# The way down of layer 0 by seven block products instead of eight, with the right operands kept in DRAM

## The chip, the core and the metric

The kernel runs on one NeuronCore of one Trainium2 chip. The time is that of one execution on the device, in microseconds (us). Three runs of the kernel before took 2002.38, 2007.29 and 2008.54 us; the median is 2007.29.

The engines are named as the profile names them: PE is TensorE (matmul), PEld its loading of the stationary operand, DVE is VectorE, ACT is ScalarE, POOL is GpSimd. SP is SyncE, whose queue (SPq) issues most of the transfers. Each engine takes its instructions strictly in the order in which the program lays them down for it.

## What is computed

Two transformer layers over x of shape (4, 512, 512), in float32. Each is x + attention(norm(x)) + ffn(norm(x)). The part that the change touches is the feed-forward half of layer 0, beside its attention, which is a scan over 32 steps of 16 tokens (test-time training: each step makes a gradient and updates the state W1 and b1).

```python
def _L0_ffn_ref(x, gate_w, up_w, down_w, gate_s, up_s, down_s):
    # here x: (2048, 512); gate_w, up_w: (1408, 512); down_w: (512, 1408)
    g = jnp.einsum('th,ih->ti', xf, gate_w) * gate_s
    u = jnp.einsum('th,ih->ti', xf, up_w) * up_s
    hdn = jax.nn.silu(g) * u
    out = jnp.einsum('ti,hi->th', hdn, down_w) * down_s
...
def step(carry, x):                      # layer 0's attention, 32 of these in a chain
    Z1 = xk @ W1_s + b1_s
    grad = _ln_fused_l2_bwd(Z1, xv - xk, ln_w, ln_b)
    ...
    W1_new = W1_s - (last_eta * xk).swapaxes(-1, -2) @ grad
```

The results must agree with this reference; the order of the sums is free.

## The kernel before

Layer 0 is one loop of 32 scan steps with other work laid between. The 2048 tokens fall into 8 chunks of 256 (CW), and a chunk holds 4 scan steps. For every chunk there is a stream of other work, the generator `between(ch)` (L656):

- `gate_up` (L465), 11 times: the inner width of 1408 is 11 tiles (NI) of 128. Each loads a gate tile and an up tile (wg, wu, 256 KB each, L471), makes 4 + 4 products of 128x256 into one PSUM bank (pf, two banks), and leaves silu(gate) x up in `hid` (ACT L477, DVE L478). `hid` has one buffer.
- the next chunk's work: `norm_turn`, `keys`, two `token_tile`s and `queries`. `token_tile` writes the step's rows to DRAM by 8 transfers each on SP (L294).
- `finish` of the chunk before: its norm, the output projection and the sum with the result of the way down.
- `down` (L483), twice, for the two halves u of 128 tokens: for each of the 11 inner tiles it loads a tile of the down weights (wd, 128x512, 256 KB, four buffers, L489) and makes one product of 512 columns, which accumulates in one PSUM bank (pd). DVE then multiplies by the row of scales `dsc` (L494), and POOL adds `brow` and x (L495, L496).

One scan step n is: `prepare` on POOL (kv fetched from DRAM, L307; sk, L314; the query part of wq_bd, L316; km, L321); on PE the products pz and then pso from wh; the gradient, a chain of some fifteen small operations on DVE with two on ACT (L356 to L390); its copies g_bd (L395, DVE and ACT), and gh on POOL (L421); then on PE the products wacc (from g_bd) and pso (from a_bd and gh), which open the next step. `fill(us)` (L702) draws pieces of `between` into the gaps of the scan by their estimated length (the numbers that the generators yield), and a step that needs a later chunk waits until that chunk's rows are made. The tile framework's planner then orders the instructions of each engine by when it expects their operands. So what stands on PE between a step's pz and its wacc or pso is fixed in the program.

In the first chunk `finish_constants` (L515) also runs: it spreads the row `dsc` over the partitions by one product of 512 columns, and makes `brow` from the output weights.

`down` and what draws it:

Of the kernel before, what the change touches and what calls it, by code (L numbers as in the profile page):

```python
# [18 lines left out]
P = 128  # L19
# [13 lines left out]
NS = 8  # L33
# [22 lines left out]
def trunk_kernel(ctx: ExitStack, tc: tile.TileContext, a: dict, out: bass.AP):  # L56
# [49 lines left out]
    with ExitStack() as px:  # L106
# [9 lines left out]
        def mm(out, lhsT, rhs, start=True, stop=True):  # L116
            nc.tensor.matmul(out, lhsT=lhsT, rhs=rhs, start=start, stop=stop, skip_group_check=True)  # L117
# [67 lines left out]
        gamma_row = wk.tile([P, HS], F32, tag="xr", name="gamma_row")  # L185
# [15 lines left out]
        tok = lrb[:, P:]  # L201


        sel8 = one.tile([NS, P], F32, tag="sel8", name="sel8")
        tok8 = one.tile([NS, 2, 4, HD], F32, tag="tok8", name="tok8")
        for h in range(2):
            r = slice(4 * h, 4 * h + 4)
            nc.gpsimd.dma_start(
# [249 lines left out]

        gs = load(one, "gs", [P, NI], eng=nc.gpsimd)
        us = load(one, "us", [P, NI], eng=nc.gpsimd)  # L460
        dsc = one.tile([P, HS], F32, tag="dsc", name="dsc")
        nc.gpsimd.dma_start(out=row["dsc"], in_=a["dsc"].unsqueeze(0))
        hid, yf = {}, {}

# [36 lines left out]
        ch8 = one.tile([NS, 4, 32], F32, tag="ch8", name="ch8")  # L501
# [12 lines left out]

        def finish_constants():  # L515
            nc.sync.dma_start(out=wo, in_=a["wo"].rearrange("(c p) o -> p c o", p=P))
            spread_row(dsc, row["dsc"])
            pt = psum()[:, :NS]
            nc.tensor.transpose(pt, ch8.rearrange("s al x -> s (al x)"), ident[:NS, :NS])
            nc.vector.tensor_copy(by_ch, pt)  # L520
            yield 1.0

            pt = psum()[:, :NC]
            mm(pt, onesd, beta_ch)
            beta_m = wk.tile([P, 1], F32, tag="beta_m", name="beta_m", bufs=1)
            nc.vector.tensor_reduce(beta_m, pt, AX.X, ALU.add)
            nc.vector.tensor_scalar(beta_ch, beta_ch, beta_m, None, ALU.subtract)

            pr = psum()
            for c in range(NC):  # L530
                pnb_b = wk.tile([P, P], F32, tag="pnb_b", name=f"pnb_b{c}")
# [1000 lines left out]
```

## Time and profile before

| | us |
|---|---|
| median of 3 runs | 2007.29 |
| profiled execution, its own time | 2001.78 |
| its span | 2000.0 |
| layer 0 (until the last latents) | about 970 to 1000 |
| layer 0's way down: 352 records of 128x512 on PE | 166.3 |
| gate and up tiles: 704 + 704 records of 128x256 | 174.7 + 168.2 |
| POOL busy, 160 to 900 us | 271.51 of 740 |
| DVE busy, 160 to 900 us | 463.55 of 740 |
| mean granted clock of PE over the span | 0.995 |

How to read it: a product in float32 leaves two records on PE, so 352 records are 176 products. A group's line gives the busy time of all its instructions, the mean of one in ns, and behind the second bar the time that its engine stood idle just before them, with what ended that wait. A line number can be that of a helper: every product of layer 0 stands at L117 (`mm`). In the views in order of time a line begins with its start and its length, and the bracket behind it holds the idle time before it.

### The profile page before, as it was taken

The numbers are of one execution on the slowest core, as the hardware profiler recorded it, in microseconds if no ns is written. First come the engines' busy times: TensorE is split into PE (matmuls) and PEld (weight loads), VectorE is DVE, ScalarE is ACT, GpSimd is POOL, SyncE is SP. The second block draws the span as 40 slices with busy tenths as digits, with TensorE's granted clock in tenths as the row PEclk, the third lists the DMA queues.
The fourth block names the chain that finished last, engine by engine and source line by source line (L and its number), as shares of the span: only waits on it lengthen the run. The fifth ranks groups of instructions, "written<-read, shape, count | busy, mean of one in ns | idle before, by whom it ended". The sixth has DMA issues, their size and how long they took to land.

```text
span 2000.0 us, 32373 instructions
## 1 busy us (share of the span) xinstructions
PE 1939.4 (97%) x11626; PEld 1233.0 (62%) x11626; DVE 1170.9 (59%) x2579; ACT 815.8 (41%) x1695; POOL 515.9 (26%) x619
## 2 busy tenths in 40 slices
PE   8999999999999999998999999999999999999997
PEld 6777676767767676743777745555555555555555
DVE  5445757475666566574555566555655556555664
ACT  2224334334334342432222165554554455445552
POOL 4334343424243343412000101111211121322110
PEclk9999999999999999999999999999999999999999
DMA  6657566646465455746652144444444434333343
GB/s 167 199 138 212 143 188 169 181 115 192 123 172 167 124 175 152 229 117 200 224 167 63 44 112 127 123 102 109 105 103 107 106 102 112 93 97 97 102 107 103
DMA packets 227307, 273.50 MB, mean 137 GB/s; under 512 B 88587, under 2 KB 117452, under 8 KB 226508
## 3 DMA queue, kind: packets, MB, share of 16 engines
q1 hardware_dynamic: 206656, 239.28, 43.5%
q0 software_dynamic: 8992, 26.84, 4.7%
q10 hardware_dynamic: 11500, 5.32, 0.9%
q8 instruction: 93, 1.52, 0.3%
q14 instruction: 66, 0.54, 0.1%
HBM read 174.18 MB, written 34.87 MB: 105 GB/s over the span
## 4 chain that ended last, share of the span: by engine, by line
PE 49%; DVE 1%; DMA 1%; SPq 0%; ACT 0%; issue 0%; DVEq 0%; ACTq 0%
PE pc L1254 11%; PE sc L1207 9%; PE pq L1184 8%; PE px L1301 5%; PE p L1301 4%; PE pk L1184 3%; PE epg L976 3%; PE epo L1039 1%; PE epu L976 1%; PE eox L1069 1%; PE pvo L891 1%; PE pw L866 1%; PE eo L1069 1%; DMA gu<-in_gu 0%; SPq L1246 0%
## 5 line engine op out<-in xcount | busy, mean ns | idle before, releaser
L1225 DVE TENSOR_REDUCE st<-sc 128x1 f32<-128x512 f32 x256 | 168.9, 681 | 242.4 <-PE sc L1207 242.4
L1227 ACT ACTIVATE prob<-sc,st 128x512 f32<-128x512 f32 x256 | 175.1, 686 | 213.7 <-DVE st L1225 213.5
L1254 PE MATMUL pc<-prT,lv 128*128 128x512 f32 x512 | 232.5, 597 | 5.2 <-DMA out<-y 3.9
L1236 DVE STREAM_TRANSPOSE tt<-prob 128x512 f32<-128x512 f32 x256 | 178.4, 700 | 46.6 <-ACT prob L1232 37.1
L1232 ACT ACTIVATE prob<-prob,st 128x512 f32<-128x512 f32 x256 | 182.0, 720 | 58.2 <-DVE st L1231 58.2
L117 PE MATMUL pf<-xT,wg 128*128 128x256 f32 x704 | 174.7, 390 | 4.1 <-DMA wg<-in_wg 2.7
L1184 PE MATMUL pq<-cq,uq 128*128 128x512 f32 x384 | 175.2, 592 | 0.0
L117 PE MATMUL pf<-xT,wu 128*128 128x256 f32 x704 | 168.2, 382 | 0.9 <-DMA wu<-in_wu 0.7
L117 PE MATMUL pd<-wd,hid 128*128 128x512 f32 x352 | 166.3, 601 | 1.3 <-DMA wd<-in_wd 1.3
L1254 PEld LDWEIGHTS pc<-prT,lv 128*128 128x128 f32 x512 | 96.8, 191 | 106.8 <-issue 104.5
L117 PEld LDWEIGHTS pf<-xT,wg 128*128 128x128 f32 x704 | 133.1, 193 | 31.2 <-issue 4.9
L1207 PE MATMUL sc<-k,q 32*128 32x512 f32 x1024 | 145.7, 617 | 2.5 <-ACT prob L1227 2.5
L117 PEld LDWEIGHTS pf<-xT,wu 128*128 128x128 f32 x704 | 134.7, 192 | 20.7 <-DMA wu<-in_wu 2.1
L478 DVE SCALAR_TENSOR_TENSOR hid<-pf,us,sg 128x256 f32<-128x256 f32 x88 | 42.0, 478 | 155.3 <-ACT sg L477 154.9
L1184 PEld LDWEIGHTS pq<-cq,uq 128*128 128x128 f32 x384 | 74.1, 193 | 90.7 <-issue 89.7
L314 POOL TENSOR_SCALAR sk<-k,m 128x256 f32<-128x256 f32 x64 | 60.3, 952 | 180.9 <-PE pz L117 168.7
L1195 POOL TENSOR_TENSOR kr<-kr,t2k 128x512 f32<-128x512 f32 x16 | 20.3, 1268 | 332.3 <-DVE t2k L1194 332.3
L421 POOL TENSOR_SCALAR gh<-grad,m 128x256 f32<-128x256 f32 x64 | 61.9, 976 | 153.2 <-DVE grad L390 131.0
L117 PEld LDWEIGHTS pd<-wd,hid 128*128 128x128 f32 x352 | 63.3, 190 | 60.4 <-issue 44.2
L1207 PEld LDWEIGHTS sc<-k,q 32*128 32x128 f32 x1024 | 48.4, 185 | 82.8 <-issue 73.2
L477 ACT ACTIVATE sg<-pf,gs 128x256 f32<-128x256 f32 x88 | 41.6, 473 | 134.8 <-PE pf L117 134.5
L1256 ACT COPY ctxT<-pc 128x512 f32<-128x512 f32 x64 | 37.4, 584 | 132.0 <-PE pc L1254 132.0
(316 smaller groups left out, 3455.2 us busy)
## 6 DMA issues: line engine op xcount, KB each, us to landing
prT<-tt SPq DMA_DIRECT2D x1016, 64.0 KB, 2.0
wd<-in_wd SPq DMA_DIRECT2D x176, 256.0 KB, 3.1
wg<-in_wg SPq DMA_DIRECT2D x88, 256.0 KB, 3.1
wu<-in_wu SPq DMA_DIRECT2D x88, 256.0 KB, 3.0
cq<-lat_d SPq DMA_DIRECT2D x48, 256.0 KB, 3.8
rows<-rows SPq DMA_DIRECT2D x128, 66.0 KB, 2.2
kv<-rows POOLq DMA_DIRECT2D x32, 264.0 KB, 4.3
gu<-in_gu SPq DMA_DIRECT2D x3, 2048.0 KB
```

What stands on the lines that cost most here:

```text
L117: nc.tensor.matmul(out, lhsT=lhsT, rhs=rhs, start=start, stop=stop, skip_group_check=True)
L314: nc.gpsimd.tensor_scalar_mul(sk[:, :, :, h, :], at(k1[ch], slice(0, P)), m2[:, h : h + 1])
L421: nc.gpsimd.tensor_scalar_mul(gh[:, :, h, :], g, m2[:, h : h + 1])
L976: nc.tensor.matmul(ps, lhsT=w[:, c, :], rhs=x[:, c], start=start and c == 0, stop=c == 1, skip_group_check=True)
L1184: nc.tensor.matmul(ps, lhsT=columns(ws[hg][w]), rhs=x, start=(i == 0), stop=(i == len(srcs) - 1))
L1207: nc.tensor.matmul(ps[h], lhsT=qk[f"q{c}"][r, i * P : (i + 1) * P], rhs=qk[f"k{c}"][r, :], start=(n == 0), stop=(n == 2),)
L1225: pin(nc.vector.tensor_reduce(mx, ps[h], AX.X, ALU.max, negate=True))
L1227: pin(nc.scalar.activation(pr, ps[h], AF.Exp, bias=mx, scale=1.0, accum_out=sm))
L1232: pin(nc.scalar.mul(pr, pr, sm))
L1236: nc.vector.transpose(out=tt[:, :, h - 2], in_=pr.rearrange("p (k kq j) -> p kq k j", kq=4, j=32))
L1254: pin(nc.tensor.matmul(pc, lhsT=lv[:, b, k, :], rhs=at[:, :, k, :], start=(k == 0), stop=(k == E - 1)))
L1301: nc.tensor.matmul(ps[:, q, :], lhsT=a[:, k, q * P : (q + 1) * P], rhs=w[:, k, :], start=start and k == 0 and q == 0, stop=k == 1, skip_gr ...
```

## The change

The product of a chunk's hidden values (256 tokens by 1408) with the down weights (1408 by 512) is cut into a 2x2 by 2x2 block product over ten of the eleven inner tiles: the tokens into two halves of 128, the inner width into two halves of 5 tiles (KH), the output columns into two halves of 256 (half). Seven block products and sums of blocks take the place of eight. The eleventh tile is done directly, in four products of 128x256.

The right operands (three blocks as they are and four of their combinations, all already times `dsc`) are made once, during the first chunk's gate/up tiles, by `down_operands`: a piece after each of tiles 1 to 6. Each piece loads 128x2x512 of the weights (SP), multiplies by `dsc` (DVE, 128x1024), makes four differences of 128x256 (POOL) and writes the seven parts to `rights_d` in DRAM (SP, three transfers). Every chunk loads the seven operands from there, 640 KB each, into two buffers.

The left operands are two sums of 128x640 made by `left_sums` after the tenth gate/up tile, and two more made in place in `hid`, all on POOL. The seven products are made one after the other; four of them add to the same PSUM bank x without clearing it, so that the bank holds the running sum that the next output block wants, and DVE adds each result to `yf`, which already holds x (loaded at the fifth tile) and `brow`.

```diff
-        def down(ch, u):
-            xr = wk.tile([P, HS], F32, tag="xr", name=f"xr_{ch}_{u}")
-            load_rows(xr, a["x"], ch, u)
-            pd = ps_dn.tile([P, HS], F32, tag="pd", name=f"pd_{ch}_{u}")
-            for i in range(NI):
-                w = wk.tile([P, HS], F32, tag="wd", name=f"wd_{ch}_{u}_{i}", bufs=4)
-                nc.sync.dma_start(out=w, in_=a["wd"][i * P : (i + 1) * P, :])
-                mm(pd, hid[ch][:, i, u * P : (u + 1) * P], w, i == 0, i == NI - 1)
-                if i in (3, 7):
-                    yield 3.43
-            t = wk.tile([P, HS], F32, tag="yf", name=f"yf_{ch}_{u}", bufs=4)
-            nc.vector.tensor_mul(t, pd, dsc)
-            nc.gpsimd.tensor_add(xr, xr, brow)
-            nc.gpsimd.tensor_add(t, t, xr)
-            yf[ch, u] = t
-            yield 2.57
+        KH, half = NI // 2, HS // 2
+        rights_d = dram.tile([7, P, KH, half], F32, tag="rights_d", name="rights_d")
+
+        def down_operands():
+            dsc = wk.tile([P, HS], F32, tag="xs", name="dsc", bufs=3)
+            spread_row(dsc, row["dsc"])
+            nc.sync.dma_start(out=last_d, in_=a["wd"][2 * KH * P :, :])
+            nc.gpsimd.tensor_mul(last_d, last_d, dsc)
+            pairs = a["wd"][: 2 * KH * P].rearrange("(k i p) o -> i p k o", k=2, i=KH)
+            for i in range(KH):
+                raw = wk.tile([P, 2, HS], F32, tag=("zb", "pn_sq")[i % 2], name=f"wd_{i}", bufs=1)
+                nc.sync.dma_start(out=raw, in_=pairs[i])
+                nc.vector.tensor_mul(raw, raw, dsc.unsqueeze(1).to_broadcast([P, 2, HS]))
+                b11, b12, b21, b22 = (raw[:, k, o : o + half] for k in range(2) for o in (0, half))
+                t = wk.tile([P, KH, half], F32, tag="wd", name=f"td_{i}")
+                nc.gpsimd.tensor_sub(t[:, 0], b12, b11)
+                nc.gpsimd.tensor_sub(t[:, 1], b22, t[:, 0])
+                nc.gpsimd.tensor_sub(t[:, 2], b22, b12)
+                nc.gpsimd.tensor_sub(t[:, 3], b21, t[:, 1])
+                nc.sync.dma_start(out=rights_d[0][:, i], in_=b11)
+                nc.sync.dma_start(
+                    out=rights_d[1:3, :, i].rearrange("j p o -> p j o"), in_=raw[:, 1].rearrange("p (j o) -> p j o", j=2)
+                )
+                nc.sync.dma_start(out=rights_d[3:, :, i].rearrange("j p o -> p j o"), in_=t[:, :4])
+                yield
...
+        def residual(ch):
+            for u in range(2):
+                t = yf[ch, u] = wk.tile([P, HS], F32, tag="yf", name=f"yf_{ch}_{u}", bufs=4)
+                load_rows(t, a["x"], ch, u)
+
+        def left_sums(ch):
+            a11, a12, a21, a22 = (
+                hid[ch][:, k * KH : (k + 1) * KH, u * P : (u + 1) * P] for u in range(2) for k in range(2)
+            )
+            s = wk.tile([P, 2, KH, P], F32, tag="hs", name=f"hs_{ch}", bufs=1)
+            nc.gpsimd.tensor_add(s[:, 0], a21, a22)
+            nc.gpsimd.tensor_sub(s[:, 1], s[:, 0], a11)
+            left[ch] = dict(a11=a11, a12=a12, a21=a21, a22=a22, s1=s[:, 0], s2=s[:, 1])
+
+        def down(ch):
+            o = left.pop(ch)
+            def add(ps, u, oh):
+                t = yf[ch, u][:, oh * half : (oh + 1) * half]
+                nc.vector.tensor_add(t, ps, t)
+            def product(ps, x, j, start, more=None):
+                w = wk.tile([P, KH, half], F32, tag="wd", name=f"wd_{ch}_{j}")
+                nc.sync.dma_start(out=w, in_=rights_d[j])
+                for k in range(KH):
+                    mm(ps, x[:, k, :], w[:, k, :], start and k == 0, k == KH - 1 and more is None)
+                if more:
+                    last(ps, *more, False)
+            def last(ps, u, oh, start):
+                mm(ps, hid[ch][:, NI - 1, u * P : (u + 1) * P], last_d[:, oh * half : (oh + 1) * half], start, True)
...
+            x = ps_dn.tile([P, HS], F32, tag="pd", name=f"pd_{ch}")[:, :half]
+            product(x, o["a11"], 0, True)
+            for u in range(2):
+                nc.gpsimd.tensor_add(yf[ch, u], yf[ch, u], brow)
+            add(x, 0, 0)
+            yield 2.16
+            p2 = bank("p2")
+            product(p2[:, 0], o["a12"], 1, True, (0, 0))
+            last(p2[:, 1], 1, 1, True)
+            nc.gpsimd.tensor_sub(o["a21"], o["a11"], o["a21"])
+            nc.gpsimd.tensor_sub(o["a12"], o["a12"], o["s2"])
+            add(p2[:, 0], 0, 0)
+            add(p2[:, 1], 1, 1)
+            yield 3.02
+            product(x, o["s2"], 4, False)
+            add(x, 0, 1)
+            yield 2.16
...
+            product(x, o["a22"], 6, False, (1, 0))
+            add(x, 1, 0)
+            yield 2.59
...
+                if ch == 0 and 0 < i <= KH + 1:
+                    next(rights, None)
+                if i == 4:
+                    residual(ch)
+                if i == NI - 2:
+                    left_sums(ch)
...
-            for u in range(2):
-                dn = down(ch, u)
-                for j in range(3):
-                    yield from take(nxt, 2)
-                    yield from take(dn, 1)
-                    yield from take(fin, 1)
+            dn = down(ch)
+            for j in range(7):
+                yield from take(nxt, 2)
+                yield from take(dn, 1)
+                yield from take(fin, 1)
```

What else moves: the spreading of `dsc` goes from `finish_constants` into the first piece of `down_operands`; some small tiles share the buffers of others (gamma_row, sel8, tok8, ch8, pnb_b), and the buffers xr and the four of wd become those of the operands.

More of the change, by code (lines that the diff above doesn't have):

```diff
@@ L184, in trunk_kernel @@
         m2 = load(one, "m2", [P, 2], eng=nc.scalar)
-        gamma_row = wk.tile([P, HS], F32, tag="xr", name="gamma_row")
+        gamma_row = wk.tile([P, HS], F32, tag="wg", name="gamma_row")
         gbeta_row = one.tile([P, HS], F32, tag="gbeta_row", name="gbeta_row")
@@ L201, in trunk_kernel @@
         tok = lrb[:, P:]
-        sel8 = one.tile([NS, P], F32, tag="sel8", name="sel8")
-        tok8 = one.tile([NS, 2, 4, HD], F32, tag="tok8", name="tok8")
+        eights = wk.tile([P, 3, P], F32, tag="pn_rs", name="eights", bufs=1)[:NS]
+        sel8, ch8 = eights[:, 0], eights[:, 2].rearrange("s (al x) -> s al x", al=4)
+        tok8 = eights[:, 1].rearrange("s (j al d) -> s j al d", j=2, al=4)
         for h in range(2):
@@ L460, in trunk_kernel @@
         us = load(one, "us", [P, NI], eng=nc.gpsimd)
-        dsc = one.tile([P, HS], F32, tag="dsc", name="dsc")
+        last_d = one.tile([P, HS], F32, tag="last_d", name="last_d")
         nc.gpsimd.dma_start(out=row["dsc"], in_=a["dsc"].unsqueeze(0))
@@ L501, in trunk_kernel @@
-        ch8 = one.tile([NS, 4, 32], F32, tag="ch8", name="ch8")
+        KH, half = NI // 2, HS // 2
[22 more added lines that the diff above has]
+                yield
@@ new lines, in trunk_kernel @@
+        rights = down_operands()
+        left = {}
+        def residual(ch):
[10 more added lines that the diff above has]
+            left[ch] = dict(a11=a11, a12=a12, a21=a21, a22=a22, s1=s[:, 0], s2=s[:, 1])
@@ new lines, in down, with bank @@
+        def down(ch):
[12 more added lines that the diff above has]
+                mm(ps, hid[ch][:, NI - 1, u * P : (u + 1) * P], last_d[:, oh * half : (oh + 1) * half], start, True)
+            def bank(nm):
+                return ps_ff.tile([P, 2, CW], F32, tag="pf", name=f"{nm}_{ch}")
+            x = ps_dn.tile([P, HS], F32, tag="pd", name=f"pd_{ch}")[:, :half]
[15 more added lines that the diff above has]
+            yield 2.16
+            p5 = bank("p5")[:, 0]
+            product(p5, o["s1"], 3, True)
+            add(p5, 0, 1)
+            add(p5, 1, 1)
+            yield 2.16
+            product(x, o["a21"], 5, False)
+            add(x, 1, 1)
+            yield 2.16
+            p3 = bank("p3")[:, 0]
+            product(p3, o["a12"], 2, True, (0, 1))
+            add(p3, 0, 1)
+            yield 2.59
+            product(x, o["a22"], 6, False, (1, 0))
+            add(x, 1, 0)
+            yield 2.59
@@ L516, in finish_constants @@
             nc.sync.dma_start(out=wo, in_=a["wo"].rearrange("(c p) o -> p c o", p=P))
-            spread_row(dsc, row["dsc"])
             pt = psum()[:, :NS]
@@ L530, in finish_constants @@
             for c in range(NC):
-                pnb_b = wk.tile([P, P], F32, tag="pnb_b", name=f"pnb_b{c}")
+                pnb_b = wk.tile([P, CW], F32, tag="sg", name=f"pnb_b{c}")[:, :P]
                 nc.vector.tensor_copy(pnb_b, pnb[:, c : c + 1].to_broadcast([P, P]))
```

## The prediction

> **What bounds the kernel now.** I read the busy times, the stages, the costliest groups, then each engine in order of time around the first chunk, and last the order in which the changed kernel, as built, issues its instructions on each engine.
>
> ```profile
> PE 1939.4 (97%) x11626; PEld 1233.0 (62%) x11626; DVE 1170.9 (59%) x2579; ACT 815.8 (41%) x1695; POOL 515.9 (26%) x619
> ```
>
> ```profile
> 160.00:900.00 740.00, 713.46 (x6037) 510.56 (x6038) 463.55 (x1083) 284.97 (x541) 271.51 (x357) 1.00 0.58 163
> ```
>
> (Columns of the stage: length, busy PE, PEld, DVE, ACT, POOL, clock, DMA share, GB/s.) Layer 0 ends near 1000 us, and TensorE is 96% busy in it: its time is TensorE's work plus TensorE's waits, in the one order in which its instructions were laid down.
>
> ```profile
> L117 PE MATMUL pf<-xT,wg 128*128 128x256 f32 x704 | 174.7, 390 | 4.1 <-DMA wg<-in_wg 2.7
> ...
> L117 PE MATMUL pf<-xT,wu 128*128 128x256 f32 x704 | 168.2, 382 | 0.9 <-DMA wu<-in_wu 0.7
> L117 PE MATMUL pd<-wd,hid 128*128 128x512 f32 x352 | 166.3, 601 | 1.3 <-DMA wd<-in_wd 1.3
> ```
>
> Every product leaves two records. So the way down is 176 products of 512 columns at 166.3/176 = 0.945 us, and one of 256 columns costs 0.478 to 0.496 us: narrow tiles lose next to nothing.
>
> ```profile
> 47.86 1.08 PE L117 MATMUL pz<-wq_bd,sk 128*32 128x128 f32 x32
> ...
> 52.84 0.59 PE L117 MATMUL pj<-by_ch,onesd 128*128 128x4 f32 x2 [2.39 <-DVE by_ch L520]
> 53.29 3.76 PE L117 MATMUL pf<-xT,wg 128*128 128x256 f32 x8
> 56.85 2.78 PE L117 MATMUL pf<-xT,wu 128*128 128x256 f32 x8
> 59.47 1.89 PE L117 MATMUL pf<-xT,wg 128*128 128x256 f32 x8
> ...
> 84.48 0.65 PE L117 MATMUL wacc<-g_bd,km 128*32 128x64 f32 x32
> ```
>
> The first scan step opens with pz; its gradient is ready at about 60.3 (VectorE's g_bd, 59.41 + 0.90), but wacc comes only at 84.48, behind eight gate/up tiles that hide the chain. After the idle 2.39 us two groups of eight records take 3.56 and 2.62 us, start to start, against 1.73: 2.7 us lost to a lower clock (mean 0.83 from 40 to 60 us).
>
> ```profile
> 49.15 1.82 POOL L314 TENSOR_SCALAR sk<-k,m 128x256 f32<-128x256 f32 x2 [7.79 <-PE pz L117]
> 50.91 1.70 POOL L316 COPY wq_bd<-q 32x256 f32<-32x256 f32 x4
> 52.56 1.14 POOL L307 DMA_DIRECT2D kv<-rows  x2
> ```
>
> ```profile
> 29.27 8.59 SPq L294 DMA_DIRECT2D rows<-rows  x16
> 41.05 0.35 SPq L471 DMA_DIRECT2D wg<-in_wg  x1
> ```
>
> GpSimd fetches the step's keys (kv, landed at 55.58); SyncE fetches the third gate tile at 41.05, long before its use.
>
> ```profile
> 252.91 1.08 PE L117 MATMUL pz<-wq_bd,sk 128*32 128x128 f32 x32
> ...
> 264.69 0.48 PE L117 MATMUL pso<-a_bd,gh 128*32 128x68 f32 x17 [2.72 <-POOL gh L421]
> ```
>
> Here only 8 us of work lies under the chain: pz is over at 253.8 and gh ready at 264.69. So a chain lasts 10.9 us, and a step with less cover makes TensorE wait for the rest.
>
> **The change, part by part.**
>
> *Products.* 176 x 0.945 = 166.3 us go; 8 x (7 x 5 + 4) = 312 of 256 columns come, at 0.478 to 0.496: 149.1 to 154.9. Start to start, without waits, the sides are 0.8650 and 0.4325 us, 152.2 against 134.9. Gain 11.4 to 17.3; I take 17, since waits are counted below.
>
> *Chunk 0, first step.* The built order puts, on GpSimd ahead of kv, the product of last_d and four subtractions of 128x256. Such a subtraction is not in the trace: half of a 128x512 one (1.285) gives 0.64, a one-input 128x256 (0.952) bounds it above; I take 0.7, nearer to the half, since like it it has two inputs. Walk, each end from the rows above and those of its kind: the row dsc is copied at 49.2 (0.69 after hid of tile 1, 48.5); last_d 50.5 (1.29); sk 52.3 (1.82); three subtractions, a copy of wq_bd (0.43), the fourth, three more copies 56.8; first kv issued 57.4 (0.57), landed 59.8 (3.0 after the start of its issue, as before); two pairs of km (2.0, 2.2) and the two other kv issues 65.0; gh 66.9 (1.85; VectorE's gradient is ready at 63.6, 3.8 after kv as before). On SyncE the third gate tile now stands behind three stores of operands that wait for the subtractions (55.5), so the planner put pso and wacc ahead of it: TensorE has nothing from 51.6 to 66.9. 15.4 instead of 2.4: **+13**.
>
> Who stands behind whom here: on SyncE the three stores (64 KB to 512 KB of 1 KB rows) wait for VectorE's product and GpSimd's last subtraction, and behind them wait the gate and up tiles, so TensorE; the copies into blocks_d behind those are wanted only in layer 1. On GpSimd the kv fetch waits behind the subtractions, behind it km and gh, and for gh TensorE. Before, nothing of layer 0's way down stood in either queue at this point. The spread of the dsc row moves forward from behind the first scan step (one product, 0.97, and one copy, 0.69): nothing by itself, as it is done either way; but VectorE's first reduction now starts at 50.5 instead of 49.0, which the later kv hides.
>
> [...]
>
> *Second step.* wacc 68, gate/up tile 2 until 74, tile 3 until 78, pz until 79.2 (the loss of clock is in these). Only tile 4 lies between it and pso. VectorE gets two 128x1024 products (1.2 each, by zb+q's 1.214) inside the chain, GpSimd eight subtractions ahead of gh: 87.5 + 2.8 + 1.9 = 92.2, TensorE free at 83.3: **+9**. *Third:* wq_bd 1.5, g_bd and gh 1.1, an up tile issued behind a store 1.1: **+4**. *Fourth:* the rest of its pz stands behind the whole chunk and two tiles of the next, then pso must wait with 0.6 us of cover: **+10** (10.9 - 0.6).
>
> *Later boundaries.* Counting the built order (0.4325 us a 256-column product) between each pz and the first user of its gradient: the eighth step has 4.0 us of cover (before 8), the twelfth 7.5 (before 16), the sixteenth 9.8: deficits 6.9 - 2.7, 3.4, 1.1: **+9**. In the others the cover is 9 us or more, as before.
>
> *Loads.* 56 loads of 640 KB in two buffers replace 176 of 256 KB in four. Bounds for one landing: 3.1 us (256 KB) and 10.3 us (1 MB, the dn row); on the line between them 6.7; at the marginal rate of the small ones (128 KB 2.0, 256 KB 3.1) 6.4; at the 278 GB/s of the busiest stage, 2 us fixed, 4.4. I take 4.7, close to the last: the wd row itself (3.1 for 256 KB) is the same tile's and stands nearer to it than the weights of layer 1. The shortest covers in the built order (0.9, 3.0, 3.0, 3.9, 4.3, 5.0...) then miss 8 us in sum (2 at 3.1, 31 at 6.7, 107 at 10.3): **+8**.
>
> *Clock.* Four waits longer than 6 us, each losing 2.7 by the row above, less the one there is: **+8**.
>
> [...]
>
> *At nothing.* The rows of x come at the fifth gate tile instead of at the way down, 256 KB a chunk as before, into the buffers of the result: what they add to is read a chunk later. The first add of a chunk on VectorE now waits for GpSimd's two adds of brow, and the gradient's operations queue behind it; GpSimd has the time of seven gate tiles for them from the second chunk on (some 24 us), and in the first brow is made just before (at 93.7 in the trace): 2.6 us there, under the products of the keys. Nine VectorE adds of 128x256 (about 0.42) for two products of 0.69 a chunk, +2.4 us; GpSimd four of 128x640 (1.6) and two of 1.3 for four of 1.3, +3.8 us. VectorE is 63% and GpSimd 37% busy from 160 to 900; the scan's products cover them. Without that cover they lengthen eight chains by up to 6 us. Layer 1 is untouched and only starts later.
>
> Sum: -17 + 13 + 9 + 4 + 10 + 9 + 8 + 8 = +44. The profiled execution has a span of 2000.0 and 1.8 around it: 2045.8. The median shown is 5.5 above that execution; I go half way: **2048**. Bounds: with each of the four waits 2 us shorter, the boundaries at the eighth step's 4, loads and clock at 2, it is -17+11+7+2+8+4+2+2 = +19 (2021 to 2026); with each 2 longer, the products at -11, the boundaries at 11 and the loads at 31 it is +83, of which I take +65 to +70 (2067 to 2077), as these are hardly met together.
>
> **Rivals.**
> - *The waits don't come*: gh and the gate tile reach TensorE as early as before, so only the products count: 2002 - 17 = 1985. For it: the 24 us between g_bd (60.3) and wacc (84.48) in the trace, a large reserve. Against: the order is fixed, pso stands ahead of the tiles, and it decides as soon as gh comes later than 53 us, where the next work stood before; kv alone is behind 4 us of new GpSimd work. 0.08.
> - *Only the first wait is real*, the lead of the scan (three steps where there was one) repaying the others: -17 + 13 + 3 + 8, about 2009. Against: the lead is credited in the walk. By it the first product of the way down starts at 126 us against 96.42, 30 later, with 5.4 us more of the scan behind it (two wacc and pso pairs 2.4, one pz and pso 2.0, nine sixteenths of a pz 1.0): some 25 lost, which is the 13 + 9 + 4 above. 0.07.
> - *The loads rule*: a landing of 6.7 us and more, so that buffers and not products pace the seven products: +44 - 8 + 31 = +67, 2069 to 2072, and at 10.3 us 2145. For it: DMA busy 0.77 to 0.93 in the chunk changes already. Against: 1.2 MB less a chunk. 0.13.
>
> My forecast has 0.72. Below 2022 lie 0.15, above 2072 some 0.07: range 2022 to 2072. Within 0.3% (6 us, what a measurement can tell) falls half of the second rival, 0.04; faster 0.09 with a little of it; slower 0.87.
>
> **What would show it.** Right: TensorE idle about 15 us before the first pso of a_bd, released by gh; 9 and 10 us at the second and fourth; the first pd product at about 126 us instead of 96; the way down near 135 to 150 us busy. Wrong: first pd before 110 us; or waits on wd of more than 20 us in sum; or layer 0 shorter than 1000 us.

## The result, and the profile after

The changed kernel took 2111.73 us (median of 4 runs, 2100.10 to 2114.38), the kernel before 2007.14 beside it (2002.38 to 2008.54): 1.0513 times as long, interval 1.0487 to 1.054. The prediction had the direction, and a sum of 44 us where 105 were measured.

Both profiles are read up to where layer 1 starts, at the first `epg` product. Two rows of busy TensorE from 0 to that moment, of the kernel before and of the changed one (columns: stretch, its length, busy PE with its records, granted clock, DMA share, GB/s):

```profile
0.00:970.48 970.48, 925.77 (x7303) 0.99 0.59 165
```

```profile
0.00:1073.46 1073.46, 928.40 (x7575) 0.94 0.53 153
```

So TensorE is busy 2.6 us longer, though it has less to multiply, and idle 145.1 us, not 44.7. With 7.6 us more in layer 1 (2110.6 - 1073.5 against 2000.0 - 970.5) this is the whole difference of the spans: 100.4 + 2.6 + 7.6 = 110.6.

The groups of TensorE in the changed kernel up to 1060 us, to be held against `pf` and `pd` of before:

```profile
L117 PE MATMUL pf<-xT,wg 128*128 128x256 f32 x704 | 172.8, 389 | 1.9 <-DVE hid L479 1.8
L117 PE MATMUL pf<-xT,wu 128*128 128x256 f32 x704 | 170.2, 385 | 4.8 <-DMA wu<-in_wu 4.8
...
L117 PE MATMUL pd<-wd,hid 128*128 128x256 f32 x240 | 62.1, 402 | 0.1
...
L117 PE MATMUL pso<-a_bd,gh 128*32 128x68 f32 x1024 | 26.1, 231 | 57.5 <-POOL gh L422 57.5
```

The same group of `pso` in the kernel before, up to 960 us:

```profile
L117 PE MATMUL pso<-a_bd,gh 128*32 128x68 f32 x1024 | 22.6, 225 | 5.8 <-POOL gh L421 5.8
```

The products of the way down hardly wait for their loads; the scan's `pso` waits 57.5 us for `gh`, 5.8 before. The largest single waits, in order of time on TensorE:

```profile
72.46 0.32 PE L117 MATMUL pso<-a_bd,gh 128*32 128x68 f32 x1 [20.92 <-POOL gh L422]
...
100.81 0.32 PE L117 MATMUL pso<-a_bd,gh 128*32 128x68 f32 x1 [11.36 <-POOL gh L422]
...
195.31 0.32 PE L117 MATMUL pso<-a_bd,gh 128*32 128x68 f32 x1 [10.84 <-POOL gh L422]
...
1073.46 5.97 PE L1061 MATMUL epg<-xe,gu 128*128 128x256 f32 x16 [33.81 <-DMA xe<-xe_d]
```

The first three are the scan steps of chunk 0 that the prediction priced. TensorE keeps to its order there: a gate tile whose fetch SyncE issued at 57.52 us had landed 4.2 us later, and the gate products that stand behind the first `pso` start only at 74.24. The last it did not have: between layer 0 and layer 1 TensorE stands for 33.8 us. GpSimd's queue shows why the operands of layer 1 are late:

```profile
49.52 2.24 POOL L492 TENSOR_TENSOR last_d<-last_d,dsc 128x512 f32<-128x512 f32 x1 [8.06 <-issue]
...
58.31 1.15 POOL L308 DMA_DIRECT2D kv<-rows  x2
...
65.17 2.06 POOL L322 TENSOR_SCALAR km<-kv,m2n 128x256 f32<-128x256 f32 x2 [5.71 <-DMA kv<-rows]
...
1043.79 0.75 POOL L1019 DMA_DIRECT2D gu<-in_gu  x1 [59.95 <-DMA xe<-xe_d]
```

In the kernel before, GpSimd and then TensorE:

```profile
911.97 0.75 POOL L934 DMA_DIRECT2D gu<-in_gu  x1
```

```profile
970.48 3.62 PE L976 MATMUL epg<-xe,gu 128*128 128x256 f32 x16
```

The fetch of the first gate weights of layer 1 (`gu`, 2 MB) and behind it the 4 MB of `xe` go out at 1043.8, 60 us after GpSimd had nothing else to do; in the kernel before they went out at 911.97, right behind the last `zb`, with 58 us of the last finish still to come. (The first three lines of the changed kernel belong to chunk 0 and are used below.)

The reason lies in where the tiles are, not in what is computed. A pool gives each tag its place when the tag is first asked for. As the kernel before was built, `zb`, `pn_sq` and `xs` were asked for last and lay at bytes 211456 to 227904 of a partition. The change uses these three tags in `down_operands`, in the first gate/up tiles, so they are asked for ahead of the scan's tiles: `xs` now begins at 163872, `zb` at 170016, `pn_sq` at 184352. In both kernels `gu_0` lies at 150912 to 167296 and `xe` at 167296 to 200064. So layer 1's operands now lie on the buffers that the last finish and the last latents use until the very end.

### The profile page after: what moved, and what is told of

Same layout as the page of the kernel before. It is cut to its first block, busy times and chain, and to the rows that moved or that the text cites. A ratio compares the mean times of both kernels' runs of the same rounds, so it can differ in the third digit from the quotient of the medians.

```text
span 2110.6 us, 32905 instructions
## 1 busy us (share of the span) xinstructions
PE 1946.4 (92%) x11898; PEld 1298.3 (62%) x11898; DVE 1198.5 (57%) x2640; ACT 826.6 (39%) x1702; POOL 566.8 (27%) x656
## 4 chain that ended last, share of the span: by engine, by line
PE 75%; DVE 8%; DMA 6%; issue 3%; POOL 3%; SPq 3%; ACT 2%; ACTq 0%; DVEq 0%; POOLq 0%
PE pj L117 13%; PE pc L1339 10%; PE pf L117 9%; PE sc L1292 8%; PE pq L1269 7%; PE px L1386 5%; PE p L1386 4%; PE epg L1061 3%; PE pk L1269 3%; PE pd L117 2%; SPq L1331 2%; PE pz L117 2%; DMA wu<-in_wu 2%; PE p L117 2%; PE epu L1061 1%
## 5 line engine op out<-in xcount | busy, mean ns | idle before, releaser
L322 POOL TENSOR_SCALAR km<-kv,m2n 128x256 f32<-128x256 f32 x64 | 60.8, 959 | 83.9 <-PE wacc L117 56.5
L117 PE MATMUL pso<-a_bd,gh 128*32 128x68 f32 x1024 | 26.1, 231 | 57.5 <-POOL gh L422 57.5
```

The costliest lines, as they stand in the source:

```text
L322: nc.gpsimd.tensor_scalar_mul(km[:, :, :, h, :], kv[:, :, 0:64].rearrange("p b (al d) -> p b al d", d=HD), m2n[:, h : h + 1])
```

## Experiments

All times are medians beside the kernel before on the same chip; a ratio is to that kernel. The three columns behind come from one profiled execution each, up to the first `epg`: TensorE's busy and idle time, and the clock lost, which is (1 - granted clock) x 20 us summed over stretches of 20 us (it counts idle time too, and its last stretch reaches past the first `epg`). The kernels ran on several chips; from one chip to another, a difference of medians and the one by the ratios part by up to 4 us, and both are given where it matters. The profiled executions of b_slots and c_dveearly lie 5 us below and 9 us above their medians, the others nearer.

| kernel | us | ratio | busy | idle | clock lost |
|---|---|---|---|---|---|
| before | 2003 to 2007 | 1 | 925.8 | 44.7 | 7.0 |
| changed | 2111.7 | 1.0513 [1.0487, 1.054] | 928.4 | 145.1 | 62.0 |
| a_slots | 2065.8 | 1.0305 [1.0279, 1.0331] | 926.4 | 111.3 | 44.8 |
| b_slots | 2027.0 | 1.011 [1.008, 1.0139] | 923.0 | 65.9 | 16.4 |
| a_noform | 2022.7 | 1.0098 [1.0068, 1.0127] | 917.3 | 76.4 | 19.2 |
| a_pipe | 2046.0 | 1.0209 [1.018, 1.0239] | 923.8 | 90.9 | 29.4 |
| a_pipe_dve | 2043.0 | 1.0201 [1.0185, 1.0218] | 924.8 | 85.8 | 26.0 |
| c_late | 2018.9 | 1.0075 [1.0061, 1.0089] | 925.6 | 59.5 | 21.2 |
| c_late_gaps | 2007.1 | 1.0022 [1.001, 1.0033] | 911.7 | 61.4 | 5.4 |
| b_gaps | 2014.5 | 1.0062 [1.0041, 1.0082] | 930.8 | 54.6 | 15.8 |
| c_fin5 | 2016.0 | 1.0062 [1.0046, 1.0079] | 921.4 | 65.0 | 17.8 |
| c_fin5b | 2014.6 | 1.0057 [1.0043, 1.0071] | 920.3 | 62.5 | 15.6 |
| c_fin6b | 2011.3 | 1.0039 [1.0024, 1.0055] | 921.3 | 58.9 | 20.6 |
| b_fin5 | 2002.4 | 0.9998 [0.9985, 1.0012] | 923.0 | 46.6 | 7.2 |
| c_noadds | 2008.6 | 1.0014 [1.0, 1.0029] | 915.2 | 60.7 | 10.8 |
| c_nosums | 1994.7 | 0.9947 [0.9928, 0.9966] | 913.3 | 45.9 | 7.2 |
| c_noboth | 1992.2 | 0.9932 [0.991, 0.9955] | 910.8 | 45.1 | 5.4 |
| c_dvesums | 2017.2 | 1.0075 [1.0054, 1.0096] | 918.4 | 62.2 | 16.0 |
| c_dveearly | 2017.6 | 1.0086 [1.0067, 1.0105] | 924.5 | 65.2 | 19.0 |
| c_dvelate | 2022.7 | 1.0107 [1.0084, 1.013] | 923.9 | 65.1 | 19.0 |

### The places: a_slots and b_slots

a_slots asks for the tags in another sequence, after the first gate/up tile. The tiles made there are never used, and no engine's order changes.

```diff
+        def places():
+            for tag, n, bufs in (
+                ("kv", B * RW, 3), ("sk", 512, 2), ("km", 512, 2), ("wh", 512, 2), ("s", NG, 2), ("xh", 256, 1),
...
+                ("u", 256, 1), ("grad", 256, 2), ("gh", 512, 2), ("zch", NG * CT, 1), ("hs", 2 * (NI // 2) * P, 1),
+                ("wd", (NI // 2) * (HS // 2), 2),
+            ):
+                wk.tile([P, n], F32, tag=tag, name=f"place_{tag}", bufs=bufs)
...
+            if (ch, i) == (0, 0):
+                places()
```

> The changed kernel with the working pool's places asked for in another sequence: the scan's tiles first, then hs and wd, and xs, zb, pn_sq last. Every engine's instructions stand in the same order as in the changed kernel. Theory (place): gu_0 and xe of layer 1 lie in the changed kernel over xs, zb, pn_sq, which layer 0 holds to its last store; moved away, the wait of 33.8 us before the first epg falls below 3 us, and with the slow clock behind it 35 to 42 us go: 2070 to 2077 us. Rival (the finish itself is late, or the transfers are too many): the wait stays above 20 us and the time above 2100.

Measured: 2065.75, 46 us less than the changed kernel's median, or 42 by the ratios (1.0305 and 1.0513); 4 us below the range given. TensorE and GpSimd at the change of layers:

```profile
1037.76 3.62 PE L1072 MATMUL epg<-xe,gu 128*128 128x256 f32 x16
```

```profile
981.74 0.75 POOL L1030 DMA_DIRECT2D gu<-in_gu  x1
```

`gu` is fetched 62 us sooner, and the first `epg` has no bracket: no wait. The gain is at or a little above the theory's 42. Of the 45.1 us between the two spans (2110.6 and 2065.5) 35.7 lie before that product and 9.4 behind it: its group of sixteen takes 3.62 us, not 5.97, and over the 22 us from its start the granted clock is 1.00, 0.74 in the changed kernel.

b_slots is the reverse, in the kernel before: the same three tags asked for right behind `sg`, and nothing else.

```diff
+            for tag, n, bufs in (("xs", HS, 3), ("zb", NC * CW, 1), ("pn_sq", NC * CW, 1)):
+                wk.tile([P, n], F32, tag=tag, name=f"place_{tag}", bufs=bufs)
```

> The kernel before, with nothing changed but that xs, zb and pn_sq get their places right behind sg, so under xe of layer 1 (gu_0 stays free early). Theory (place): xe, 4 MB, is fetched only after the last finish, TensorE waits 12 to 25 us before the first epg, and the time is 2019 to 2035 us without any of the new work. Rival (the wait belongs to the new work): 2007 us, no wait.

Measured: 2027.04, 24 us above the kernel before, whose work and order it has to the last instruction. Its first `epg`:

```profile
988.88 5.11 PE L982 MATMUL epg<-xe,gu 128*128 128x256 f32 x16 [20.77 <-DMA xe<-xe_d]
```

The wait appears without any block product. The theory of the places is shown from both sides; the rival is out.

### Forming the right operands: a_noform, a_pipe, a_pipe_dve

a_noform forms nothing: each product's 640 KB come from `wd` itself. Without `down_operands` the tags fall into the sequence of a_slots by themselves, so a_slots is what to compare with.

```diff
-        rights_d = dram.tile([7, P, KH, half], F32, tag="rights_d", name="rights_d")
+        flat_wd = a["wd"].rearrange("r o -> (r o)")
+        rights_d = [flat_wd[j % 2 * 5 * P * 256 :][: P * KH * half].rearrange("(p k o) -> p k o", p=P, k=KH) for j in range(7)]
...
-                if ch == 0 and 0 < i <= KH + 1:
-                    next(rights, None)
+                if (ch, i) == (0, 1):
+                    nc.sync.dma_start(out=last_d, in_=a["wd"][2 * KH * P :, :])
```

> The changed kernel without forming right operands: the products read 640 KB slices of wd itself (the values are left out, the scale too), last_d is loaded and not scaled. The places fall behind the scan's as in a_slots. Theory (forming): a_slots less the 45 to 53 us of chunk 0, so 2018 to 2030 us; the wait before the first pso of a_bd below 4 us. Rival (the seven products, their adds and loads cost it): above 2050 us.

Measured: 2022.65, 43 us below a_slots. The first `pso` of `a_bd` no longer waits. GpSimd's queue shows where: chunk 0's results `z` went out at 215.8 us in a_slots and at 172.3 here. So forming costs 43 us, all in chunk 0. But 19 us over the kernel before are left, although seven products stand in place of eight: that is followed up below.

a_pipe parts the forming into three steps a gate tile apart, so that SyncE meets a store only when its operand is long made.

```diff
+            for n in range(KH + 2):
+                if n > 1:
+                    i, raw, t = n - 2, raws.pop(n - 2), tds.pop(n - 2)
+                    nc.sync.dma_start(out=rights_d[0][:, i], in_=raw[:, 0, :half])
...
+                if 0 < n <= KH:
+                    nc.vector.tensor_mul(raw, raw, dsc.unsqueeze(1).to_broadcast([P, 2, HS]))
...
+                if n < KH:
+                    nc.sync.dma_start(out=raws[n], in_=pairs[n])
+                yield
```

> a_slots with the forming of right operands in three steps, one gate tile apart: load, then product and subtractions, then the three stores. Theory (SyncE: the stores that wait for subtractions hold the gate tiles): 15 to 35 us below a_slots, 2038 to 2058. Rival (GpSimd: the subtractions ahead of kv hold gh, which this leaves): within 8 us of a_slots.

Measured: 2046.03, 20 us below a_slots, inside the theory's range: SyncE's stores that stand ahead of the gate tiles are a good part of the 43. The planner now lays gate tiles under the first chains again, and the long waits of chunk 0 are 11.7, 2.3, 3.5 and 5.7 us. `kv` is still issued at 57.0.

a_pipe_dve moves the twenty subtractions to VectorE, four like this one for each piece:

```diff
-                    nc.gpsimd.tensor_sub(t[:, 0], b12, b11)
+                    nc.vector.tensor_sub(t[:, 0], b12, b11)
```

> a_pipe with the twenty subtractions on VectorE in place of GpSimd. Theory (on GpSimd they stand ahead of kv and gh): kv is issued 3 us sooner, the waits of the first two steps shrink, 5 to 15 us below a_pipe. Rival (what is missing there is products over the chain, and VectorE, which has the chain itself, gets 9 us more): same as a_pipe within 4 us, or slower.

Measured: 2042.98, 3 us below a_pipe (2 by the ratios): the rival's answer. But the theory's condition did not come about: `kv` is issued at 57.04, in a_pipe at 56.99, since the product of `last_d` starts at 50.98 here and at 48.20 there. So moving the subtractions wins next to nothing, and what an earlier `kv` would win is not shown.

### Forming under chunk 0's own way down: c_late, c_late_gaps, b_gaps

c_late gives chunk 0 whole products. A pair of `wd` tiles is loaded once, scaled, multiplied by both token halves, and then formed and stored; so the work is not ahead of the first scan steps.

```diff
+            for i in range(KH):
+                for u in range(2):
+                    for k in range(2):
+                        mm(pds[u], hid[0][:, k * KH + i, u * P : (u + 1) * P], raws[i][:, k], i + k == 0, False)
+                formed(i)
+                if i > 0:
+                    stored(i - 1)
...
+                yield 3.43
...
-            dn = down(ch)
+            dn = down(ch) if ch else rights
```

> a_slots with chunk 0's way down by whole products again (each pair of wd tiles is loaded once, scaled, multiplied, and then formed into right operands under those products), so that nothing of it stands in the first scan steps; chunks 1 to 7 use the seven products. Theory (forming hurts only where it is ahead of the first steps): the waits of 20.4, 11.5 and 10.9 us go; counted by the order in which the products stand, the short covers miss 8 us in sum instead of 40: 2010 to 2022 us. Rival (forming costs by its transfers and by GpSimd wherever it is put): 2033 us or more.

Measured: 2018.87, inside the theory's range and 27 us below a_pipe; by the ratios (1.0075 and 1.0098) it is even 5 us below a_noform, which forms nothing. The forming's stores and sums are all still there, so most of its cost was where they stood. (The run also has chunk 0's whole products, and scales `last_d` on VectorE.)

c_late_gaps changes the constants that say how much work is laid under the three parts of a scan step; b_gaps does the same to the kernel before.

```diff
-GAPS, LAST_GAPS = (11.0, 3.0, 8.0), (10.0, 3.0, 7.0)
+GAPS, LAST_GAPS = (11.0, 3.0, 7.5), (10.0, 3.0, 6.5)
```

> c_late with other constants for how much work is laid under a scan step: (11, 3, 7.5) for (11, 3, 8), in the last chunk (10, 3, 6.5) for (10, 3, 7). Theory (a chunk's way down got shorter by 2 us, so the old constants use it up too early, and steps 8 and 12 and the last finish lack cover): the short covers fall from 8 us to 1 in sum, 13 us more products are left for the last finish, 10 to 20 us less than c_late, 1990 to 2005. Rival (the idle time comes from the sums and adds on VectorE and GpSimd that the seven products need): within 4 us of c_late.

> The kernel before with the constants of c_late_gaps and nothing else: what the constants alone do. Theory (they fit the shorter way down only): within 5 us of before, or slower, since a cover of 5.8 us stands at step 29. Rival (they are better for any kernel): 5 us or more faster than before, and then a gain of c_late_gaps isn't the products'.

Measured: 2007.1 for c_late_gaps, 12 us less than c_late (the gain that was expected, though the time lies 2 us above the range given), and 2014.46 for b_gaps, slower than the kernel before. So the constants suit the shorter way down alone. The two rows of busy TensorE, c_late and c_late_gaps, with one count of records:

```profile
0.00:985.08 985.08, 925.55 (x7542) 0.98 0.54 156
```

```profile
0.00:973.13 973.13, 911.73 (x7542) 0.99 0.55 158
```

The same products take 13.8 us less of TensorE's time, and the idle time is no shorter (59.5 and 61.4). It was the clock: 21.2 us lost in one, 5.4 in the other. So the gain came in about the size that the theory gave and not by its way, which is partly luck: up to 900 us the waits for `gh` did fall, from 11.0 to 6.7, but others grew by as much. And c_late_gaps against before, at nearly one clock, gives the price of the seven products: 925.8 - 911.7 = 14.1 us for seven chunks. But its idle time is 16.7 us longer, so nothing is won.

### What takes the 14 us: c_fin5, c_fin5b, c_fin6b, b_fin5

In c_late_gaps `pd` waits 4.8 us for VectorE's adds, and the finish's products wait 8 us for VectorE's `pn_sq`. The finish's four reciprocals (1.75 us each) stand there right ahead of the block sums. These runs take the finish's first piece earlier:

```diff
-                if i == NI - 3:
+                if i == NI - 5:
                     yield from take(fin, 1)
```

c_fin5b also moves GpSimd's two sums of `yf` and `brow` out of `down`:

```diff
+                if i == NI - 4 and ch:
+                    for u in range(2):
+                        nc.gpsimd.tensor_add(yf[ch, u], yf[ch, u], brow)
```

c_fin6b takes the piece at `NI - 6`; b_fin5 is the control.

> c_late_gaps with the first piece of the previous chunk's finish (four reciprocals of 1.75 us and their products on VectorE) taken at the seventh gate tile of a chunk in place of the ninth, where VectorE is idle. Theory (the seven products lose what they gain because their sums stand on VectorE behind that piece, so the bank pd stays taken): the waits of pd on yf (L580) fall from 5 us to under 2, those of pj on pn_sq (L669) from 8 to under 4, and 4 to 12 us go: 1995 to 2003 us. Rival (VectorE is short of time as such): the waits only move, within 3 us of 2007.

> c_fin5 with GpSimd's two sums of yf and brow at the eighth gate tile, not inside the first product, so that the first add of a chunk has only the product to wait for. Theory (GpSimd's sums release the first add): 1 to 4 us below c_fin5. Rival (VectorE's own queue does): the same as c_fin5 within 2 us.

> c_fin5b with the finish's first piece one gate tile earlier still, the sixth. Theory (the earlier, the less stands before the sums): the same or up to 3 us less. Rival (the row of z has not landed yet, and its square holds ScalarE and with it the gate tiles): slower by 3 us or more.

> The kernel before with the finish's first piece at the seventh gate tile and nothing else: the control of c_fin5. Theory (before, pd is drained twice a chunk and not nine times, so VectorE's order matters little): within 4 us of before. Rival (a gain that has nothing to do with the seven products): 4 us or more faster.

Measured: 2016.04, 2014.63, 2011.26, and 2002.39 for the control (no change, as its theory had it). In c_fin5 the waits of `pd` are gone as expected, and the time is 9 us longer: the finish's `pj` now waits for ScalarE's square instead (9.5 us up to 900 us, 4.5 in c_late_gaps), those on VectorE's `pn_sq` stay at 8.3, and 12 us more of the clock are lost. The theory fell; the waits only moved, as the rival had it, but not within its 3 us. The three runs part by 1 to 5 us, and single times of c_fin6b by 15 (2004 to 2019), so the theories of c_fin5b and c_fin6b are not decided.

### Leaving the sums out: c_noadds, c_nosums, c_noboth

c_noadds leaves out eight of VectorE's nine adds a chunk (first lines of the diff), c_nosums GpSimd's four sums of left operands (the others), c_noboth both.

```diff
-                nc.vector.tensor_add(t, ps, t)
+                if (u, oh) == (1, 0):
...
+                    nc.vector.tensor_add(t, ps, t)
...
-            s = wk.tile([P, 2, KH, P], F32, tag="hs", name=f"hs_{ch}", bufs=1)
-            nc.gpsimd.tensor_add(s[:, 0], a21, a22)
-            nc.gpsimd.tensor_sub(s[:, 1], s[:, 0], a11)
...
-            nc.gpsimd.tensor_sub(o["a21"], o["a11"], o["a21"])
-            nc.gpsimd.tensor_sub(o["a12"], o["a12"], o["s2"])
```

> c_late_gaps without eight of the nine adds by which VectorE takes the block products into yf in each of chunks 1 to 7 (these values are left out): the products stand as before, but no product waits for a bank. Theory (VectorE's sums eat the gain: they hold pd and stand inside the scan's chain and the finish): 8 to 14 us less than c_late_gaps, 1993 to 1999. Rival (what eats it is the order of the products, with waits at other places, and the clock): within 4 us of c_late_gaps.

> c_late_gaps without GpSimd's four sums of left operands a chunk (1.55 us each); the products read hid where they read the sums. Theory (GpSimd's sums hold gh, sk and wq_bd of the scan, and the products of s2): 4 to 10 us less than c_late_gaps. Rival (GpSimd has room): within 3 us of it.

> Both left out, the adds on VectorE and the sums on GpSimd: what the seven products alone would bring. Theory (the sums as a whole eat it): 10 to 18 us less than c_late_gaps, 1989 to 1997, so the 14 us of products come through. Rival (order and clock): within 4 us of c_late_gaps.

Measured: 2008.55, 1994.69, 1992.23, against 2007.1. Without VectorE's adds nothing is won that can be measured (part of TensorE's order is new there). Without GpSimd's sums 12.4 us are won, 15 by the ratios, more than the 4 to 10 expected; and in c_nosums, as built, every engine has all its other instructions in the order of c_late_gaps, so the gain is the sums' and no new order's. With both away the seven products show in full:

```profile
0.00:955.84 955.84, 910.75 (x7542) 0.99 0.57 161
```

15.0 us less busy than before, 0.4 us more idle.

What GpSimd's sums do beside holding their own queue can be seen on VectorE. GpSimd, then VectorE, in c_late_gaps:

```profile
305.33 1.55 POOL L605 TENSOR_TENSOR hid<-hid 128x640 f32<-128x640 f32 x1
```

```profile
305.55 1.61 DVE L686 SCALAR_TENSOR_TENSOR zb<-zb,by_ch,pn_rs 128x256 f32<-128x256 f32 x1
...
309.05 0.47 DVE L686 SCALAR_TENSOR_TENSOR zb<-zb,by_ch,pn_rs 128x256 f32<-128x256 f32 x1
```

The same instruction takes 1.61 us when it starts 0.2 us after the start of such a sum, and ends 0.3 us after it; alone it takes 0.47. Over 160 to 900 us, c_late_gaps and then c_nosums:

```profile
L686 DVE SCALAR_TENSOR_TENSOR zb<-zb,by_ch,pn_rs 128x256 f32<-128x256 f32 x28 | 19.5, 695 | 0.1
```

```profile
L681 DVE SCALAR_TENSOR_TENSOR zb<-zb,by_ch,pn_rs 128x256 f32<-128x256 f32 x28 | 13.5, 483 | 0.1
```

The rows show that the instruction takes longer beside a sum, not what holds it.

How much of the sums' cost comes by way of VectorE can be read from TensorE's waits. The finish's first products up to 950 us, c_late_gaps and then c_nosums:

```profile
L117 PE MATMUL pj<-pn_sq,onesd 128*128 128x256 f32 x16 | 5.8, 447 | 8.2 <-DVE pn_sq L669 8.2
```

```profile
L117 PE MATMUL pj<-pn_sq,onesd 128*128 128x256 f32 x16 | 5.1, 401 | 2.3 <-DVE pn_sq L664 2.3
```

Those for VectorE's `pn_sq` fall by 5.9 us; those of `pd` for its `yf` fall from 4.8 to 1.0 and those of `wacc` for its `g_bd` from 4.2 to 0.6. Together that is 13.3 us, where all idle time falls by 15.5. The waits for GpSimd's own `gh` fall by only 3.3, from 6.7 to 3.4. So the greater part of what the sums cost reaches TensorE through VectorE; how much of that is VectorE's instructions taking longer beside a sum, and how much VectorE's own waits for GpSimd's results, is not shown apart.

### The sums on VectorE: c_dvesums, c_dveearly, c_dvelate

All four sums of c_late_gaps go to VectorE, or the first two, or the last two:

```diff
-            nc.gpsimd.tensor_add(s[:, 0], a21, a22)
-            nc.gpsimd.tensor_sub(s[:, 1], s[:, 0], a11)
+            nc.vector.tensor_add(s[:, 0], a21, a22)
+            nc.vector.tensor_sub(s[:, 1], s[:, 0], a11)
...
-            nc.gpsimd.tensor_sub(o["a21"], o["a11"], o["a21"])
-            nc.gpsimd.tensor_sub(o["a12"], o["a12"], o["s2"])
+            nc.vector.tensor_sub(o["a21"], o["a11"], o["a21"])
+            nc.vector.tensor_sub(o["a12"], o["a12"], o["s2"])
```

> c_late_gaps with the four sums of left operands on VectorE, not GpSimd. In c_late_gaps VectorE's product of zb takes 0.96 us on average where a GpSimd sum runs beside it and 0.47 where none does. Theory (GpSimd's two-input sums cost twice: they hold GpSimd's own queue and stop VectorE while they run): 5 to 12 us below c_late_gaps, 1995 to 2002, faster than before; VectorE's zb product back at 0.48. Rival (VectorE gets 3 to 4 us more a chunk at the place where its chain, the finish and the sums meet; a cover of 3.8 us stands at step 25): 2004 or more.

> c_late_gaps with the first two sums (hs) on VectorE, the two into hid on GpSimd. Theory: 2 to 8 us below c_late_gaps, since half of the overlap goes; rival: the same within 2 us.

> c_late_gaps with the first two sums (hs) on GpSimd, the two into hid on VectorE. Theory: 2 to 8 us below c_late_gaps, without the short cover that c_dvesums has at step 25; rival: the same within 2 us.

Measured: 2017.22, 2017.62, 2022.73, all slower than c_late_gaps. In c_dvesums VectorE's product of `zb` is back at 0.487 us, as expected, and a sum takes 0.80 to 0.85 us, not 1.55. But up to 900 us `pso` waits 12.5 us for `gh` (6.7 in c_late_gaps) and `wacc` 7.8 for `g_bd` (6.1), while the waits for `yf` and `pn_sq` are shorter. In sum the idle time is only 0.8 us longer; 6.7 us are TensorE's busy time, with 16.0 us of clock lost where c_late_gaps lost 5.4. So the sums on VectorE end the overlap, but the scan's chain comes later, and 10.6 us more of the clock are lost. The planner also orders TensorE anew in each of these, so how much is the sums' own time and how much the new order stays open. No form that computes the whole result is faster than the kernel before; c_late_gaps, the best one, is 0.22% slower.

## Why the prediction was wrong

It had the direction, the places of the waits in chunk 0 and the worth of the products. It missed by 64 us, and its range by 40. Point by point, by its own steps:

- **Products, -17: right.** 14.1 us over seven chunks (c_late_gaps against before) are 16 for eight. The sign given for it, a way down 135 to 150 us busy, was a bad one: the groups sum to 163.4, and to 160.6 in a_noform, since the busy time of a group of ten records holds its ends, which overlap what follows: the group at 152.20 us of the changed kernel is put at 2.32 us, and the next row begins 2.16 us after its start.
- **Chunk 0, +13, +9, +4, +10: mechanism right, size short.** Waits of 20.9, 11.4, 1.8 and 10.8 us stand in the trace, 42.5 more than the 2.4 of before, where 36 were forecast; the first `pd` product came at 139.5, not 126. The first wait is 5.5 us longer than the walk had it, and two of its terms make 5.4 of that. GpSimd began to issue `kv` at 58.3, not at 56.8: its product of `last_d` took 2.24 us, not 1.29, beside a product of VectorE that had begun 0.1 us before it. And the landing of `kv`, taken as 3.0 us, was 6.9 up to the `km` that waits for it; the median landing between 40 and 75 us was 4.9, 3.2 before (over the whole run 3.9 and 4.3). In those microseconds SyncE let go a store of 512 KB, four gate and up tiles and a load of 512 KB, and the DMA engines were 89 to 100% busy from 58 to 64 us. That these held `kv` is likely; no run shows it alone.
- **Later boundaries, +9: about 7.** The eighth step's wait is 7.35 us (2.72 before), the twelfth's 2.8 (none).
- **Loads, +8: not there.** The products wait 0.1 us for `wd` (1.3 before); the landing is 4.2 us, not 4.7. (The 2 us taken as fixed are what a transfer of 64 KB takes in the kernel before: 2.0, the median of 1016 `prT`.) Gate and up tiles wait 4.8 us for their loads, 3.4 before.
- **Clock, +8: mis-sized, about 23.** The products left in layer 0 at the clock of before would be busy 925.8 - 16 = 910; it was 928.4, so 19, and 4 more in layer 1 (1018.0 against 1013.6). The step charged four long waits; but a short one cost as well (1.7 us behind a wait of 2.26 in c_late, below), and the wait at the change of layers was not among them.
- **At nothing, VectorE and GpSimd, up to 6 us without cover: too small.** Up to the change of layers TensorE waits 22 us for VectorE's `hid`, `yf`, `pn_sq` and `x`, 3.5 before: 18. In c_late_gaps GpSimd's four sums alone cost 12 us (c_nosums); the step counted their time on GpSimd, not what VectorE's instructions lose beside them (`zb` takes 1.61 us, not 0.47).
- **"Layer 1 is untouched and only starts later": this is the step that failed.** It put the change of layers at nothing; 33.8 us of waiting stand there, and 42 to 46 us went when a_slots moved the places. The built order was read engine by engine, but not what each tile lies on: that the fetch of `gu_0` had come to wait for VectorE and ScalarE stood in the program. With this step alone put right (a_slots) the time is 2065.75, inside the range; that it would have been inside owes something to luck, as the clock and VectorE's waits were too small and the loads too large. None of the signs given for being wrong appears in the trace, so they did not cover this step.

With what was measured the sum is -16 + 42.5 + 7 + 0 + 23 + 18 + 34 = 108.5, against 110.6 between the spans.

Of the rivals none came true. *The loads rule* is refuted by the landing and the waits on `wd`; *only the first wait is real* by the second, third and fourth; *the waits don't come* by the first.

## What to carry to other kernels

Ask what a new or earlier tile does to the places of all others: a buffer asked for sooner can push long-lived tiles under the next stage's operands, and the stall appears some 1000 us away from the edit (33.8 us, here). Work that is made once belongs under the work that uses it first, not ahead of the chain that opens the kernel (c_late is 27 us below a_pipe), and not in one piece where a queue holds the next stage's loads behind its stores (a_pipe is 20 us below a_slots). A cheaper product is worth its saving only if its sums, the constants of the plan and the clock leave the chain beside it as it was: in c_late_gaps 14.1 us of busy time were saved, and 16.7 us of idle time came in their place.

## What the runs showed of the hardware

In c_late 1.7 us of clock were lost behind a wait of 2.26 us. Two rows of c_late, the same product after nearly the same wait, and the stretch behind the second:

```profile
531.61 1.97 PE L117 MATMUL pd<-wd,hs 128*128 128x256 f32 x8 [2.23 <-DVE yf L580]
...
640.95 2.44 PE L117 MATMUL pd<-wd,hs 128*128 128x256 f32 x8 [2.26 <-DVE yf L580]
```

```profile
642.00:644.00 2.00, 2.00 (x7) 0.58 0.02 8
```

After the wait of 2.26 us that ends at 640.95 the clock is 1.00 up to 642, then 0.58 and 0.57 in two stretches of 2 us, a loss of 1.7 us, and 1.00 behind them up to 652; after the one that ends at 531.61 it is 1.00 in every stretch up to 538. In the kernel before, around the wait of 2.72 us that ends at 264.69 it is 1.00 in every stretch from 260 to 272; around the one of 2.39 us that ends at 52.84 it is 0.50 from 52 to 58. So among these four the length of the wait does not decide it; what does is not shown. Up to the first `epg`, c_late has 30 stretches of 2 us with a clock under 0.95 and c_late_gaps 9: it lost 16 us more clock at 1.9 us less idle time.
